# Layer-norm sources transposed in halves beside the projection lanes, and score maxima turned by products with the identity

## The chip, the cores and the metric

The kernel runs on one core of a Trainium2 chip. The metric is the time of one execution on the device in microseconds. The engines are called by their names in the profile: PE (TensorE), PEld (its weight loads), DVE (VectorE), ACT (ScalarE), POOL (GpSimd), SP (SyncE, which here only issues DMAs). All times are in microseconds where nothing else is said.

## The reference

One transformer block (PixArt) over a batch of 16, with 256 tokens and 256 features, 16 heads of 16 features:

```python
c_proj = silu(c) @ W_mod + b_mod
shift_a, scale_a, gate_a, shift_m, scale_m, gate_m = split(c_proj, 6)
q, k, v = heads(modulate(ln(x), shift_a, scale_a) @ W_qkv + b_qkv)
a = softmax(q @ k.T * hd ** -0.5) @ v
x = x + gate_a * (a @ W_proj + b_proj)
q_c = heads(ln(x) @ W_qc + b_qc)
k_c, v_c = heads(ln(context) @ W_kvc + b_kvc)
x = x + (softmax(q_c @ k_c.T * hd ** -0.5) @ v_c) @ W_cproj + b_cproj
h = gelu(modulate(ln(x), shift_m, scale_m) @ W_mlp1 + b_mlp1)
x = x + gate_m * (h @ W_mlp2 + b_mlp2)
```

Everything is float32. Most products split an operand into a rounded high part and a low remainder (both fp32r) and add three products.

## The kernel before, in words

The work after a set-up is 32 attention **units** (lines 790 to 805), 16 of self attention (kind "s") and 16 of cross attention (kind "c"). The first five and every second one up to number 25 are self attention, the others, and the last five, are cross attention. After them comes the MLP, which the change doesn't touch.

Each unit is done in eight **beats**; `beat(n, k)` (line 1103) writes out, engine by engine, what beat k of unit n issues. The order on every engine is the order of the program. PE's work in a beat:

- `visit` (line 1079): first the scores of the *next* unit (tile `s`, two pairs of matmuls of 63 rows, which sit in the two row halves of the array and run side by side). DVE takes their row maxima with one reduction (`s_tile`, line 697). There are two banks for the scores, and both are filled in each beat. Then the scores of this unit, turned (tile `st`, two pairs with 64 rows, `t_part`), which ACT exponentiates into `pt` (`exp`, line 752). Row 63 of `q` holds the negated maxima, so that `st` is already reduced by them.
- In beats 0, 2, 4 and 6 the values: `av_part` (line 771), eight products with 32 columns each, float32, that go to four column groups of the array.
- In beats 1, 3, 5 and 7 twelve pairs of projection steps, `lanes` (line 471): two matmuls side by side, one in each row half, for two projections (of Q, K, V of later units and the output projection of an earlier one). Each projection needs two lanes, one of each half, in two different beats.
- In between the transposes. `transposed` (line 377) turns a normalized source of 256 tokens by four whole-array transposes of 128 by 128, two for each half of the features. `m_turn` (line 728) turns 16 columns of maxima by one transpose, ACT negates and copies them (`m_row`, line 735), and one DMA on SP writes them into row 63 of `q`.

So a unit's maxima are turned in two halves, in beat 4 of the unit before it and in its own beat 0. The source of unit n + 3 is turned in beat 0 (two transposes, in one bank with the maxima) and beat 2 (two). Where unit n + 3 is a cross unit, its second source (`psT_q`) has all four in beat 4, and the maxima use bank `st`.

Three PSUM banks of tag "tr" go round (line 67): in a unit they serve in turn the source, a projection, the values, the second source or the maxima, a projection, the values. A fourth ("gen") holds projections by tokens, and two pairs hold `s` and `st`.

DVE's order in a beat is the maximum, then the remainders: l_k or l_kc in beat 0, l_q or l_qc in beat 4 (`low`, line 507), `xTl_s` in beat 3, `xTl_q` in beat 7, and the statistics of the layer norms. On SP in beat 0 stand the high parts of K, then the pull of the sums `S`, then the maxima, then the low part of K; in beat 4 the high parts of Q, the maxima, the low part of Q.

All instructions are recorded under line 51 of the profile, since a helper issues them. They are told apart by their tiles.

Of the kernel before, what the change touches and what calls it, by code (L numbers as in the profile page):

```python
# [10 lines left out]
F32 = mybir.dt.float32  # L11
F32R = mybir.dt.float32r
AF = mybir.ActivationFunctionType
ALU = mybir.AluOpType
# [7 lines left out]
def pixart_block(  # L22
# [53 lines left out]
    DVE.memset(wz, 0.0)  # L76
    ident = const.tile([P, P], F32, name="ident")
    make_identity(nc, ident)
    mhalf = const.tile([P, 2], F32, name="mhalf")
    POOL.memset(mhalf, -0.5)  # L80

    def gap(pool, n, name):

        pool.tile([P, n // 4], F32, tag=name, name=name, bufs=1)
# [292 lines left out]
    def transposed(src, name, scale=None, pool=False):  # L377

        o = Box()

        def place():
            o.ps = ps_gen(f"psT_{name}", SHORT)

        def turn(fs=range(KC)):
            if len(fs) == KC:
                place()
            for f in fs:
                for t in range(NT):
                    PE.transpose(o.ps[:, f * N + t * P:f * N + (t + 1) * P],
                                 src()[:, t, f * P:(f + 1) * P], ident)  # L390

        def high():
            hi = work.tile([P, KC, N], F32R, tag="xTh", name=f"xTh_{name}", bufs=4)
            lo = work.tile([P, KC, N], F32R, tag="xTl", name=f"xTl_{name}", bufs=4)
            o.xT = (hi, lo)
            if scale is None:
                ACT.copy(hi.rearrange("p k n -> p (k n)"), o.ps)
            else:
                for f in range(KC):
                    ACT.activation(hi[:, f], o.ps[:, f * N:(f + 1) * N], AF.Identity, scale=scale[f])  # L400

        def low():
            hi, lo = o.xT
            if scale is None:
                DVE.tensor_tensor(lo.rearrange("p k n -> p (k n)"), o.ps,
                                  hi.rearrange("p k n -> p (k n)"), ALU.subtract)
            else:
                for f in range(KC):
                    DVE.scalar_tensor_tensor(lo[:, f], o.ps[:, f * N:(f + 1) * N], scale[f],
                                             hi[:, f], ALU.mult, ALU.subtract)  # L410

        def full():
            o.y = work.tile([P, KC, N], F32, tag="y", name=f"y_{name}", bufs=1)
            if scale is None:
                ACT.copy(o.y.rearrange("p k n -> p (k n)"), o.ps)
            else:
# [54 lines left out]
    def lanes(x, y):  # L471


        if x:
            x.ps, x.fresh = ps_gen(f"ps_{x.name}", LONG if x.tok else SHORT), True
        return zip_longest(*(lane(o, half) for half, o in enumerate((x, y)) if o))

    def run(steps, n=12):
        for _ in islice(steps, n):
# [2 lines left out]
    def to_stack(W, src, bias, dst, which, name):  # L482
# [24 lines left out]
        def low():  # L507
            if name == "k0":
                gap(work, 64, "gap_l")
            o.lo = work.tile([P, KC, N], F32R, tag="qkl", name=f"l_{name}", bufs=3)  # L510
            if name == "k0":
                gap(work, 192, "gap_mx")
            for f in range(KC):
                DVE.scalar_tensor_tensor(o.lo[:, f], o.ps[:, f * N:(f + 1) * N], bias[f], o.hi[:, f],
                                         ALU.add, ALU.subtract)
# [181 lines left out]
    def s_tile(u, g, par, t, bank=None, home=sp):  # L697
# [12 lines left out]
            if j == 0:  # L710
                yield
        if u.mx is None:
            u.mx = work.tile([P, 2, 2, 4, NT], F32, tag="mx", name=f"mx_{u.n}", bufs=3)
# [14 lines left out]
    def m_turn(u, hf, pst=None):  # L728

        if pst is None:  # L730
            pst = ps_gen(f"psm_{u.n}_{hf}", SHORT)
        PE.transpose(pst[:16, :P], u.mx[:, hf].rearrange("p r a t -> p (r a t)"), ident)
        return pst

    def m_row(u, hf, pst):

# [31 lines left out]
            for f in pieces:  # L768
                next(f)

    def av_part(u, g):
# [8 lines left out]
        if g == 3:  # L780
            o_out(u, 1)

    def o_out(u, half):
# [295 lines left out]
    def visit(n, k, home=sp, between=None):  # L1079
# [13 lines left out]
        in_turn(*t)  # L1093
        later.append(lambda: exp(units[n], k))

    def spare(n, gate=True):
        p1, _, p3 = (v and v.post for v in map(unit, (n - 1, n - 2, n - 3)))
        if p3 and not p3.added:
            p3.add()
        if p1 and gate:  # L1100
            p1.gate()

    def beat(n, k):
# [20 lines left out]
        if k == 6:  # L1124
            if q2 and not n:
                q2.V.keep()
            if p2 and not alone:
                p2.end()
        kp = None
        if k == 5 and lx and n:  # L1130
            kp = lanes(q3.K, None if alone else p2)
        visit(n, k, between=kp and (lambda: run(kp, 2)))
        if k == 0:
            exps()
            if prev:
                av_part(prev, 3)
            if q3 and q3.ready:
                q3.T[0].place()
                pst = m_turn(cur, 1, q3.T[0].ps[:, N:])
                q3.T[0].turn((0,))  # L1140
            else:
                pst = m_turn(cur, 1)
            if prev:
                p1.pull_sums(1)
            m_row(cur, 1, pst)
            if q2:
                q2.K.low()
                q2.K.send_low()
# [3 lines left out]
                p2.low()  # L1152
        elif k == 1:
            exps()
            run(lanes(q2 and q2.Q, q2 and n and q2.V))
            if prev:
                p1.pull_values(1)
            if lc:
# [6 lines left out]
        elif k == 2:  # L1165
            exps()
            if cur:
                av_part(cur, 0)
            if q3:
                q3.T[0].turn((1,) if q3.ready else (0, 1))  # L1170
            if ls:
                ls.ln[0].steps[0]()
            elif prev:
# [24 lines left out]
        elif k == 4:  # L1198
            exps()
            if alone:  # L1200
                p2.end()
            if cur:
                av_part(cur, 1)
            if lx:
                lx.T[1].turn()
            if nxt:
                m_part(nxt, 0, st[:, 0] if lx else None)
            if q2:
                q2.Q.low()
                q2.Q.send_low()  # L1210
# [7 lines left out]
                ls.ready = True  # L1218
        elif k == 5:
            exps()  # L1220
            run(kp or lanes(q3 and q3.K, (None if alone else p2) if n else q2.V))
            if cur:
                o_out(cur, 0)
            if lc:
# [8 lines left out]
        elif k == 6:  # L1233
# [6 lines left out]
                cur.post.pull(0)  # L1240
            if q3 and p2:
                q3.vk = lanes(q3.V, q3.K)
                run(q3.vk, 1)
            if p3:
                p3.store()
            if lx:
# [126 lines left out]
```

## Time and profile before

| | us |
|---|---|
| median of 3 runs | 719.43 |
| lowest and highest run | 718.43, 721.32 |
| span of the profiled execution | 719.7 |
| PE busy | 710.4 |
| DVE busy | 567.8 |
| ACT busy | 551.7 |
| POOL busy | 520.6 |

The span is the time from the first to the last instruction of the execution that was profiled; it is the only time that this execution has, and it lies within the three runs. PE's ends are modelled, so its 99% does not say that it is at its peak. A row of the timeline is: start, time, engine, line, operation, out<-in, shapes, count, and in brackets the idle time before it. A form such as 64*128 is the part of the array that a matmul uses, rows by columns: 63*128 and 64*128 are half the rows, 128*32 a quarter of the columns, 128*128 the whole. The matmuls of a row that stands for several have started one after another; a pair in two row halves starts nearly together.

### The profile page before, as it was taken

The numbers are of one execution on the slowest core, as the hardware profiler recorded it, in microseconds if no ns is written. First come the engines' busy times: TensorE is split into PE (matmuls) and PEld (weight loads), VectorE is DVE, ScalarE is ACT, GpSimd is POOL, SyncE is SP. The second block draws the span as 40 slices with busy tenths as digits, with TensorE's granted clock in tenths as the row PEclk, the third lists the DMA queues.
The fourth block names the chain that finished last, engine by engine and source line by source line (L and its number), as shares of the span: only waits on it lengthen the run. The fifth ranks groups of instructions, "written<-read, shape, count | busy, mean of one in ns | idle before, by whom it ended". The sixth has DMA issues, their size and how long they took to land.

```text
span 719.7 us, 22488 instructions
## 1 busy us (share of the span) xinstructions
PE 710.4 (99%) x8993; PEld 592.3 (82%) x8993; DVE 567.8 (79%) x895; ACT 551.7 (77%) x955; POOL 520.6 (72%) x518
## 2 busy tenths in 40 slices
PE   9999999999999999999999999999999999999997
PEld 8777777777877778777787777777779999999997
DVE  5878888888888798888888888888675777777653
ACT  5677888888888788887888888887867677666661
POOL 7655778787776867776686798977857988656651
PEclk9999999999999999999999999999999999999999
DMA  7574455554545456454655656456323132313212
GB/s 236 183 233 157 160 170 178 175 179 160 167 151 196 162 176 191 163 166 153 195 167 176 210 174 195 156 192 196 95 78 103 59 87 61 88 46 88 66 39 74
DMA packets 81548, 106.15 MB, mean 147 GB/s; under 512 B 16610, under 2 KB 44548, under 8 KB 81444
## 3 DMA queue, kind: packets, MB, share of 16 engines
q1 hardware_dynamic: 80548, 104.37, 45.5%
q8 instruction: 71, 1.16, 0.7%
q10 hardware_dynamic: 896, 0.35, 0.2%
q14 instruction: 33, 0.27, 0.1%
HBM read 35.89 MB, written 8.98 MB: 62 GB/s over the span
## 4 chain that ended last, share of the span: by engine, by line
PE 94%; DVE 3%; POOL 2%; issue 0%; ACT 0%; POOLq 0%; ACTq 0%
PE s L51 18%; PE o L51 16%; PE st L51 16%; PE ph L51 12%; PE ps_qc L51 4%; PE ps_kc L51 4%; PE ps_k L51 4%; PE ps_q L51 3%; PE ps_v_c L51 3%; PE ps_v_s L51 3%; PE ps_P_s L51 2%; DVE mx L51 2%; PE ps_P_c L51 2%; PE psT_c L51 2%; PE psT_s L51 2%; PE psT_q L51 1%
## 5 line engine op out<-in xcount | busy, mean ns | idle before, releaser
L51 DVE TENSOR_REDUCE mx<-s 128x4 f32<-128x1024 f32 x252 | 307.9, 1222 | 73.5 <-PE s L51 70.1
L51 ACT ACTIVATE pt<-st 128x1024 f32<-128x1024 f32 x256 | 263.4, 1029 | 51.8 <-PE st L51 51.0
L51 PE MATMUL o<-pt,v 128*32 128x256 f32 x2048 | 137.1, 385 | 0.0
L51 PE MATMUL s<-big 63*128 63x256 f32 x1008 | 116.8, 305 | 1.7 <-DVE st_q L51 0.8
L51 PE MATMUL st<-big 64*128 64x256 f32 (+1 forms) x1040 | 107.7, 282 | 0.8 <-issue 0.4
L51 PE MATMUL ph<-xTh_m,wself 128*128 128x256 f32 x512 | 100.2, 281 | 0.0
L51 POOL TENSOR_TENSOR hl<-hf,hh 128x512 fp32r<-128x512 f32 x60 | 80.1, 1350 | 20.8 <-ACT hh L51 20.8
L51 PEld LDWEIGHTS s<-big 63*128 63x128 f32 x1008 | 77.3, 185 | 21.0 <-issue 7.1
L51 PEld LDWEIGHTS o<-pt,v 128*32 128x32 f32 x2048 | 53.4, 109 | 39.5 <-ACT oT L51 1.3
L51 PEld LDWEIGHTS st<-big 64*128 64x128 f32 (+1 forms) x1040 | 81.2, 186 | 3.6 <-ACT pt L51 1.5
L51 PEld LDWEIGHTS ph<-xTh_m,wself 128*128 128x128 f32 x512 | 82.3, 188 | 1.2 <-issue 0.4
L51 PE MATMUL ph<-xTl_m,wself 128*128 128x256 f32 x256 | 71.1, 278 | 0.0
L51 ACT ACTIVATE hf<-ph,bT 128x256 f32<-128x256 f32 x112 | 47.0, 473 | 22.1 <-PE ph L51 21.9
L51 ACT ACTIVATE hh<-ph,bT 128x256 fp32r<-128x256 f32 x112 | 47.0, 472 | 19.8 <-PE st L51 8.4
L51 PEld LDWEIGHTS ph<-xTl_m,wself 128*128 128x128 f32 x256 | 48.2, 188 | 0.0
L51 PE MATMUL s<-big,hh 128*128 128x256 f32 x256 | 45.6, 278 | 0.0
L51 DVE TENSOR_SCALAR xn_m<-x,mv_m,rs_m 128x256 f32<-128x256 f32 x28 | 33.5, 1237 | 14.8 <-POOL rs_m L51 14.8
L51 POOL TENSOR_SCALAR xn_q<-x,mv_q,rs_q 128x256 f32<-128x256 f32 x32 | 38.9, 1225 | 1.7
L51 POOL TENSOR_SCALAR xn_c<-c,mv_c,rs_c 128x256 f32<-128x256 f32 x32 | 38.9, 1226 | 1.7
L51 PE MATMUL st<-big,hh 128*128 128x256 f32 x224 | 40.0, 278 | 0.0
L51 PEld LDWEIGHTS s<-big,hh 128*128 128x128 f32 x256 | 38.8, 188 | 0.0
L51 POOL TENSOR_SCALAR rs_c<-mv_c 128x2 f32<-128x2 f32 x16 | 3.6, 228 | 48.3 <-DVE mv_c L51 48.2
(230 smaller groups left out, 2133.1 us busy)
## 6 DMA issues: line engine op xcount, KB each, us to landing
big<-h_k SPq DMA_DIRECT2D x32, 256.0 KB
big<-h_kc SPq DMA_DIRECT2D x32, 256.0 KB
big<-h_qc SPq DMA_DIRECT2D x32, 256.0 KB
big<-h_q SPq DMA_DIRECT2D x30, 256.0 KB
big<-l_k SPq DMA_DIRECT2D x16, 256.0 KB
g<-gd SPq DMA_DIRECT2D x16, 256.0 KB
U_s<-oT SPq DMA_DIRECT2D x32, 128.0 KB
R_s<-rd_s SPq DMA_DIRECT2D x16, 256.0 KB
```

Of the source, the lines that this page charges most:

```text
L51: i = f(*a, **k)
```

## The change

It does five things.

1. `half(h)` of a source: four transposes of 64 tokens by 128 features, in one row half of the array, instead of whole ones. `turning` issues four of them with two steps of the lane that uses the other row half: transpose, lane, transpose, transpose, lane, transpose.
2. The first half of a source stands at the head of beat 1 (second source: beat 5), ahead of the scores; the second half between `s` and `st` of the next beat. The lanes of beat 1 and 5 then run ten pairs. In beat 5 of such units no pairs stand between `s` and `st` any more.
3. The maxima are turned by `m_cols`: two products with the identity, with 32 columns (16 of them zero), ahead of the values in beats 0 and 4. They go into the bank of the source that is turned next, where there is one.
4. `m_send`: DVE negates and copies 64 by 64 of them, and two DMAs of 64 queries each write them, ahead of the copy of the values and the pull of the sums.
5. Where the second source is turned, beat 6 issues no pair of the next lanes after the values (before: one), and beat 7 all twelve.

The tile of maxima becomes a fixed one of 32 columns, cleared once, and a gap in memory is widened so that what follows stays in place. Unit 0's source stays as it was.

```diff
+    mxs = const.tile([P, 3, 2, 32], F32, name="mxs")
+    POOL.memset(mxs, 0.0)
+    mxs = [mxs[:, i] for i in range(3)]
...
+        def half(h):
+            rows = slice(64 * h, 64 * h + 64)
+            for f in range(KC):
+                for t in range(NT):
+                    c = f * N + t * P + 64 * h
+                    PE.transpose(o.ps[:, c:c + 64], src()[rows, t, f * P:(f + 1) * P], ident[rows, rows])
+                    yield
...
+    def pair_of(x, y):
+        return [lane(o, half) if o else iter(()) for half, o in enumerate((x, y))]
+    def turning(T, h, beside):
+        t = T.half(h)
+        for f in (t, beside, t, t, beside, t):
+            next(f)
...
-                gap(work, 192, "gap_mx")
+                gap(work, 576, "gap_mx")
...
+    def m_cols(u, hf, pst=None):
+        if pst is None:
+            pst = ps_gen(f"psm_{u.n}_{hf}", SHORT)
+        w = mxs[u.n % 3][:, hf]
+        for j in range(2):
+            PE.matmul(pst[32 * j:32 * j + 32, :64], w, ident[:, 64 * j:64 * j + 64], start=True, stop=True,
+                      tile_position=(0, 32 * j))
+        return pst
+    def m_send(u, hf, pst):
+        m = work.tile([64, 64], F32R, tag="m2", name=f"m2_{u.n}_{hf}", bufs=1)
+        DVE.tensor_scalar(m, pst[:64, :64], -1.0, None, ALU.mult)
+        for j in range(2):
+            SP.dma_start(u.q[63:P:64, 4 * hf:4 * hf + 4].rearrange("r a (t q) -> r a t q", t=NT)[..., 64 * j:64 * j + 64].bitcast(F32),
+                         m[32 * j:32 * j + 16].bitcast(F32))
...
-        kp = None
-        if k == 5 and lx and n:
-            kp = lanes(q3.K, None if alone else p2)
-        visit(n, k, between=kp and (lambda: run(kp, 2)))
+        between = None
+        if k in (1, 5):
+            x, y, T = ((q2 and q2.Q, q2 and n and q2.V, q3 and q3.ready and q3.T[0]) if k == 1 else
+                       (q3 and q3.K, (None if alone else p2) if n else q2.V, lx and lx.T[1]))
+            if x:
+                x.ps, x.fresh = ps_gen(f"ps_{x.name}", LONG if x.tok else SHORT), True
+            a, b = pair_of(x, y)
+            steps = weave(a, b)
+            if T:
+                held.append((T, a))
+                turning(T, 0, b)
+        elif held:
+            between = lambda: turning(held[0][0], 1, held.pop()[1])
+        visit(n, k, between=between)
+        def rest_of():
+            run(steps, 10 if held else 12)
         if k == 0:
             exps()
+            T = q3 and q3.ready and q3.T[0]
+            if T:
+                T.place()
+            pst = m_cols(cur, 1, T.ps if T else None)
             if prev:
-                av_part(prev, 3)
-            if q3 and q3.ready:
-                q3.T[0].place()
-                pst = m_turn(cur, 1, q3.T[0].ps[:, N:])
-                q3.T[0].turn((0,))
-            else:
-                pst = m_turn(cur, 1)
+                av_part(prev, 3, False)
+            m_send(cur, 1, pst)
             if prev:
+                o_out(prev, 1)
                 p1.pull_sums(1)
-            m_row(cur, 1, pst)
...
-            if q3:
-                q3.T[0].turn((1,) if q3.ready else (0, 1))
+            if q3 and not q3.ready:
+                q3.T[0].turn()
...
+            if lx:
+                lx.T[1].place()
+            if nxt:
+                pst = m_cols(nxt, 0, lx.T[1].ps if lx else None)
             if cur:
                 av_part(cur, 1)
-            if lx:
-                lx.T[1].turn()
             if nxt:
-                m_part(nxt, 0, st[:, 0] if lx else None)
+                m_send(nxt, 0, pst)
...
-                run(q3.vk, 1)
+                run(q3.vk, 0 if lx else 1)
```

More of the change, by code (lines that the diff above doesn't have):

```diff
@@ L390, in turn @@
                                  src()[:, t, f * P:(f + 1) * P], ident)
+        def half(h):
[5 more added lines that the diff above has]
+                    yield
+        o.half = half
         def high():
@@ L475, in lanes, with weave @@
             x.ps, x.fresh = ps_gen(f"ps_{x.name}", LONG if x.tok else SHORT), True
-        return zip_longest(*(lane(o, half) for half, o in enumerate((x, y)) if o))
+        return weave(*pair_of(x, y))
+    def pair_of(x, y):
+        return [lane(o, half) if o else iter(()) for half, o in enumerate((x, y))]
+    def weave(*gens):
+        return zip_longest(*gens)
+    def turning(T, h, beside):
+        t = T.half(h)
+        for f in (t, beside, t, t, beside, t):
+            next(f)
     def run(steps, n=12):
@@ L712, in s_tile @@
         if u.mx is None:
-            u.mx = work.tile([P, 2, 2, 4, NT], F32, tag="mx", name=f"mx_{u.n}", bufs=3)
+            u.mx = mxs[u.n % 3][:, :, :16].rearrange("p f (r a t) -> p f r a t", r=2, t=NT)
         mx = u.mx.rearrange("p f r a t -> p r f a t")
@@ L769, in in_turn, with av_part @@
                 next(f)
-    def av_part(u, g):
+    def av_part(u, g, out=True):
         if g % 2 == 0:
@@ L779, in av_part @@
                           start=(c == 0), stop=(c == NT - 1), tile_position=(0, h * 32))
-        if g == 3:
+        if g == 3 and out:
             o_out(u, 1)
@@ L1094, in visit @@
         later.append(lambda: exp(units[n], k))
+    held = []
     def spare(n, gate=True):
@@ L1154, in beat @@
             exps()
-            run(lanes(q2 and q2.Q, q2 and n and q2.V))
+            rest_of()
             if prev:
@@ L1220, in beat @@
             exps()
-            run(kp or lanes(q3 and q3.K, (None if alone else p2) if n else q2.V))
+            rest_of()
             if cur:
```

## The prediction

> **What bounds the kernel now.** I read the page first, then the timeline of TensorE through two units in the steady part, then the timelines of VectorE and of the weight loads beside it.
>
> ```profile
> span 719.7 us, 22488 instructions
> ...
> PE 710.4 (99%) x8993; PEld 592.3 (82%) x8993; DVE 567.8 (79%) x895; ACT 551.7 (77%) x955; POOL 520.6 (72%) x518
> ...
> PE 94%; DVE 3%; POOL 2%; issue 0%; ACT 0%; POOLq 0%; ACTq 0%
> ```
>
> TensorE is busy 99% of the span, and the chain is 94% TensorE. But ends of matmuls are modelled, so what a beat costs must be read from start to start. That is what the timeline of TensorE gives. Beats 1 to 7 of one unit whose look-ahead unit is a cross one (a "c unit" below, 16 of them), then beat 0 of the next unit, then beats 4 and 5 of that next one (an "s unit", 12 of them with the early transposes):
>
> ```profile
> 300.93 0.51 PE L51 MATMUL s<-big 63*128 63x256 f32 x4
> ...
> 302.93 0.43 PE L51 MATMUL s<-big 63*128 63x256 f32 x4
> 303.17 0.42 PE L51 MATMUL st<-big 64*128 64x256 f32 x4
> 303.52 1.07 PE L51 MATMUL o<-pt,v 128*32 128x256 f32 x16
> 304.53 0.44 PE L51 MATMUL psT_c<-ident,xn_c 128*128 128x128 f32 x2
> 304.90 0.50 PE L51 MATMUL s<-big 63*128 63x256 f32 x4
> 305.24 0.41 PE L51 MATMUL st<-big 64*128 64x256 f32 x4
> 306.85 0.42 PE L51 MATMUL s<-big 63*128 63x256 f32 x4
> 307.43 1.07 PE L51 MATMUL o<-pt,v 128*32 128x256 f32 x16
> ...
> 309.16 0.51 PE L51 MATMUL s<-big 63*128 63x256 f32 x4
> ...
> 311.11 0.42 PE L51 MATMUL s<-big 63*128 63x256 f32 x4
> 311.73 1.07 PE L51 MATMUL o<-pt,v 128*32 128x256 f32 x16
> 312.96 0.40 PE L51 MATMUL s<-big 63*128 63x256 f32 x4
> ...
> 314.74 0.45 PE L51 MATMUL s<-big 63*128 63x256 f32 x4
> 315.35 1.07 PE L51 MATMUL o<-pt,v 128*32 128x256 f32 x16
> ...
> 316.78 0.50 PE L51 MATMUL s<-big 63*128 63x256 f32 x4
> ...
> 322.72 0.41 PE L51 MATMUL s<-big 63*128 63x256 f32 x4
> 323.30 1.07 PE L51 MATMUL o<-pt,v 128*32 128x256 f32 x16
> 324.51 0.51 PE L51 MATMUL s<-big 63*128 63x256 f32 x4
> ...
> 326.47 0.44 PE L51 MATMUL s<-big 63*128 63x256 f32 x4
> ```
>
> A beat runs from one group of scores (s) to the next. So now: beat 0 is 314.74 to 316.78, 2.04; beat 1 2.00; beat 2 1.97; beat 3 1.95; beat 4 2.31 in a c unit and 1.79 in an s unit; beat 5 1.95; beat 6 1.85; beat 7 1.78. Beats with a whole-array transpose are long because the array changes its form twice. The last four value products of beat 2, and the same place in beat 6 where no transpose follows:
>
> ```profile
> 304.20 0.40 PE L51 MATMUL o<-pt,v 128*32 128x256 f32 x4
> ```
> ```profile
> 312.73 0.38 PE L51 MATMUL ps_v_c<-wvch,xTh_c 64*128 64x256 f32 x1
> ```
>
> From 304.20 to the transpose are 0.33, to the scores another 0.37. In beat 6 the values start at 311.73 and the next half-array product comes 1.00 later, as the transpose does from 303.52 to 304.53 (1.01): leaving the values costs 0.33 whatever follows. A transpose between them is therefore paid in full, with its second change of form.
>
> The second bound is behind it:
>
> ```profile
> 314.68 0.30 PEld L51 LDWEIGHTS s<-big 63*128 63x128 f32 x4
> ```
> ```profile
> 313.40 1.23 DVE L51 TENSOR_REDUCE mx<-s 128x4 f32<-128x1024 f32 x1 [0.61 <-PE s L51]
> ...
> 315.23 1.22 DVE L51 TENSOR_REDUCE mx<-s 128x4 f32<-128x1024 f32 x1
> 316.37 0.87 DVE L51 SCALAR_TENSOR_TENSOR l_kc<-ps_kc,bP,h_kc 128x256 fp32r<-128x256 f32 x2
> ```
>
> The maximum ends at 313.40 + 1.23 = 314.63 and the next scores' weights load 0.05 later, the matmul at 314.74. The two score banks are free only then. So no beat can be shorter than scores to maximum 0.44, the maximum 1.23, load and start 0.11: 1.78, and 1.85 in beat 6; I take 1.81 as the **floor**. Beats 6 and 7 stand on it now.
>
> **The change part by part.** Only starts count. One settled pair of half-array products takes 0.115: from 305.24 to 306.85 are fourteen.
>
> *Removed.* The two half-transposes at beats 0 and 2, the four of beat 4 in c units, the maxima's transpose at beats 0 and 4: with them the second change of form.
>
> *Moved in, the turnings* (line 389's transposes in halves): each is four transposes of 64 columns with two products of the other lane, once at the head of beats 1 (and 5 in c units), once between scores and second scores of beats 2 (and 6). The trace shows no such form. Nearest are whole transposes among products of the late part, where no form changes:
>
> ```profile
> 548.60 0.28 PE L51 MATMUL s<-big,hl 128*128 128x256 f32 x1
> 548.72 0.60 PE L51 MATMUL psT_m<-ident,xn_m 128*128 128x128 f32 x4
> 549.08 0.36 PE L51 MATMUL ph<-xTh_m,wself 128*128 128x256 f32 x1
> 549.28 0.28 PE L51 MATMUL ph<-xTl_m,wself 128*128 128x256 f32 x1
> ```
>
> Six starts from 548.60 to 549.28: 0.11 each, so a transpose of 128 columns costs 0.11 and mixing costs nothing; half the columns 0.055, four 0.22. Two products take 0.23 on the other half. Lower end: 0.23, the transposes all beside the products. At the head the first weight load is bare, as after every change of form (304.90 to 305.24 is 0.34, settled 302.93 to 303.17 is 0.24): 0.10 + 0.23 = **0.34** in place of that bare load at the scores; between the scores **0.26**, since one transpose trails. Upper end: each transpose with its own load, 0.45. The two products taken from beats 1 and 5 shorten those by 0.23.
>
> *Added, maxima as products*: two products with 32 columns, in the form of the values, ahead of them. The change into that form (0.35 after the second scores' start) is paid already. The price is unseen. The values' load is the row for it:
>
> ```profile
> L51 PEld LDWEIGHTS o<-pt,v 128*32 128x32 f32 x2048 | 53.4, 109 | 39.5 <-ACT oT L51 1.3
> L51 DVE SCALAR_TENSOR_TENSOR l_k<-ps_k,bqkv,h_k 128x256 fp32r<-128x256 f32 x32 | 13.9, 475 | 0.0
> L51 DVE SCALAR_TENSOR_TENSOR bqkv<-st,bP 128x32 f32<-128x32 f32 x2 | 0.4, 191 | 0.7 <-PE st L51 0.7
> ```
>
> Sixteen matmuls stand for eight products, so each runs in two passes: two loads of 0.11, **0.23**; ends 0.11 (a quarter of the values' columns) and 0.44 (four bare loads).
>
> *Moved, the copy* of the maxima from ScalarE to VectorE, between the maximum and l_k or l_q. 32 columns take 0.19, 256 take 0.475; 64 by a line between them: **0.23**, ends 0.19 and 0.475. Successive VectorE work overlaps by 0.08 (316.37 against 315.23 + 1.22), so its occupancy is 0.15. It adds a wait: the maxima now lie in the bank the turning writes, so the turning at the head of beat 1 or 5 waits for the copy, and every score behind it in TensorE's order.
>
> *Queues.* Each half's row goes out in two DMAs instead of one on SP; they now stand ahead of the sums' pull, and l_k and l_q leave later by one more issue, about 0.55 by this row:
>
> ```profile
> 310.86 0.54 SPq L51 DMA_DIRECT2D big<-l_q  x1
> ```
>
> l_q is needed by the scores at 314.74, 3.3 after its issue ended; 2.8 are left, and no TensorE row here waits for a DMA. The maxima are needed four beats later. I cost both at nothing; without that slack it would be 0.55 a unit. ScalarE gives up 0.27 twice a unit, off the path; POOL gets one early memset.
>
> *Sum by beat, c unit.* Beat 0: scores to values 0.61, maxima 0.23, values and change 1.01: the turning could start at 1.85. The maximum starts at 0.49, ends at 1.71, the copy at 1.71 - 0.08 + 0.23 = 1.86, seen at 1.91. Plus 0.34: 2.25, **+0.21**. Beat 1: fourteen pairs, 1.61, below the floor: 1.81, **-0.19**. Here the gain is capped: VectorE's maximum is late next. Beat 2: 0.59 + 0.26 + 1.01 = 1.86, **-0.11**. Beat 3 unchanged. Beat 4: 0.58 + 0.23 + 1.01 = 1.82; with 0.44 from scores to maximum the copy is seen at 1.86; plus 0.34: 2.20, **-0.11**. Beat 5: on the floor, **-0.14**. Beat 6: loses its pair of products, gains a turning: 0.58 + 0.26 + 1.01 = 1.85, **0**. Beat 7: twelve pairs now and a bare load, like beat 3, 1.95: **+0.17**. Together -0.17.
>
> *s unit.* Beats 0 to 2 as above, -0.09. Beats 4 and 5 hang on VectorE:
>
> ```profile
> 323.21 1.22 DVE L51 TENSOR_REDUCE mx<-s 128x4 f32<-128x1024 f32 x1
> 324.35 0.87 DVE L51 SCALAR_TENSOR_TENSOR l_qc<-ps_qc,bP,h_qc 128x256 fp32r<-128x256 f32 x2
> 325.13 1.21 DVE L51 TENSOR_REDUCE mx<-s 128x4 f32<-128x1024 f32 x1
> ```
>
> These stand end to end, and the scores at 326.47 follow 325.13 + 1.21 by 0.13: the copy pushes them by 0.15. The products at beat 4 also need the bank that VectorE reads last just ahead of 323.21 (until 323.21 + 0.08 = 323.29); they would start at 323.30, so 0.05 of waiting at most, under the same VectorE chain. Together +0.06.
>
> 16 x -0.17 + 12 x 0.06 = -2.0 us. The profiled execution's span is 719.7, which gives 717.7; the median of the runs shown is 719.43, 0.3 lower, so I forecast **717.4**.
>
> **The rivals.** *The turnings don't run beside the products* (slower). If a transpose's load can't go under a running matmul of its own half, each takes load and stream and the turning 0.45: +0.11 at beats 0 and 4, +0.19 at 2 and 6; 16 x 0.60 + 12 x 0.30 = 13.2, so **730.5**. It decides from 0.064 a turning (88 of them make the 5.6 us from forecast to slower by 0.5%). Against it: the 0.11 of whole transposes in one form, which leaves no room for a bare load. For it: no row has four loads in one half between products of the other. The Trainium skill, page TensorE: Matmul & The Clock Gate, Part 3, "What overlaps and what doesn't", says that a weight load overlaps running matmuls only where the row group differs; by that rule the time would be that 730.5. The rows at 548.72 disagree for the whole array, and no run here shows halves.
>
> *The copy is dear* (slower): at 0.475 the wait grows by 0.25 in beats 0 and 4 of c units and in beats 0 and 5 of s units, 16 x 0.50 + 12 x 0.50 = 14: **731.5**. The 32-column row speaks against it.
>
> *The transposes vanish beside the products* (faster): head 0.23, between 0.23, copy 0.19: c units gain 2 x 0.11 + 2 x 0.03 + 2 x 0.04, s units 0.11 + 0.03 + 2 x 0.04: 16 x 0.36 + 12 x 0.22 = 8.4: **709**. The bare load at 304.90 speaks against the whole of it. Below that the floor stands.
>
> **How the numbers follow.** Forecast 0.40, hidden transposes 0.34, turnings in series 0.19, dear copy 0.07. About 0.5% (3.6 us) is what a measurement can tell from no change. Faster by more: the third rival, 0.34; same: the forecast less a little spill to slower, 0.38; slower 0.28. Range for 8 in 10: 709 to 728, which takes the faster rival and turnings that are partly serial. The forecast's own range is 714.5 to 721.5.
>
> **What would show it.** Right: beat 1 at 1.81 with the scores' load 0.05 behind the maximum; beat 0 near 2.25 with the first half-transpose waiting for VectorE's copy; beat 7 of c units at 1.95; no 128*128 form left in the loop's steady part. Wrong: four half-transposes more than 0.34 from first start to the scores; the maxima's products over 0.3; a copy over 0.3; scores waiting for a DMA.

## The result, and the profile after

The changed kernel takes 722.99 us (median of 7 runs, 721.09 to 725.32), the kernel before beside it 719.43 us (7 runs). The ratio is 1.0048, with a 95% interval of 1.0031 to 1.0066: slower by a little less than 0.5%, where 717.4 us had been forecast. The time lies inside the range of 709 to 728, but on the other side of the kernel before.

The page of the changed kernel, with the lines that answer to those shown of before:

```profile
span 720.7 us, 23403 instructions
...
PE 701.6 (97%) x9358; PEld 599.6 (83%) x9358; DVE 574.8 (80%) x958; ACT 542.9 (75%) x892; POOL 520.8 (72%) x519
...
PE 73%; issue 7%; POOL 7%; DVE 7%; DMA 3%; ACT 1%; SPq 1%; DVEq 0%; ACTq 0%; POOLq 0%
```

The profiled execution took 722.46 us. TensorE's busy time went down by 8.8 us and the span did not, so time has moved from work into waits; the chain, 94% TensorE before, now leaves it for a quarter of its way. Which waits these are, the waits of the weight loads and of TensorE tell (columns: us in total, times, longest us). First the kernel before, then the changed kernel:

```profile
PEld s L51 <- DVE mx L51: 5.4, 14, 0.6
```
```profile
PEld s L51 <- DVE mxs L51: 27.1, 63, 0.6
```
```profile
PE psT_c L51 <- DVE m L51: 3.0, 15, 0.2
PE psT_q L51 <- DVE m L51: 2.8, 14, 0.2
PE psT_s L51 <- DVE m L51: 1.8, 9, 0.2
```

The scores' weights wait for the maximum 63 times instead of 14: more beats stand on the floor. And the first half-transpose waits for VectorE's copy `m`, 15 + 14 + 9 = 38 times. The timeline of TensorE through beats 0, 1 and 2 of a c unit of the changed kernel shows both places:

```profile
302.01 0.42 PE L51 MATMUL s<-big 63*128 63x256 f32 x4
302.26 0.40 PE L51 MATMUL st<-big 64*128 64x256 f32 x4
302.59 0.25 PE L51 MATMUL psT_c<-ident,mxs 128*32 128x64 f32 x2
...
302.73 1.03 PE L51 MATMUL o<-pt,v 128*32 128x256 f32 x14
303.96 0.24 PE L51 MATMUL psT_c<-ident,xn_c 64*128 64x64 f32 x1 [0.20 <-DVE m L51]
...
304.21 0.50 PE L51 MATMUL s<-big 63*128 63x256 f32 x4
304.53 0.42 PE L51 MATMUL st<-big 64*128 64x256 f32 x4
...
306.02 0.51 PE L51 MATMUL s<-big 63*128 63x256 f32 x4
306.37 0.28 PE L51 MATMUL ps_q<-xTl_s,wself 64*128 64x256 f32 x1
306.37 0.28 PE L51 MATMUL psT_c<-ident,xn_c 64*128 64x64 f32 x2
...
306.59 0.48 PE L51 MATMUL st<-big 64*128 64x256 f32 x4
307.00 1.07 PE L51 MATMUL o<-pt,v 128*32 128x256 f32 x16
308.00 0.50 PE L51 MATMUL s<-big 63*128 63x256 f32 x4
```

Beat 0 (302.01 to 304.21) is 2.20, beat 1 1.81, beat 2 1.98. Over all units, the medians of each beat from the first start of its scores to that of the next (16 c units, 12 s units; the last column belongs to an experiment below):

| beat | c before | c forecast | c after | s before | s after | c, copy on ScalarE where a turning follows |
|---|---|---|---|---|---|---|
| 0 | 2.06 | 2.25 | 2.24 | 2.04 | 2.22 | 2.02 |
| 1 | 1.99 | 1.81 | 1.82 | 2.00 | 1.82 | 1.82 |
| 2 | 1.97 | 1.86 | 1.97 | 1.95 | 1.97 | 1.97 |
| 3 | 1.95 | 1.95 | 1.97 | 1.95 | 1.96 | 1.96 |
| 4 | 2.31 | 2.20 | 2.19 | 1.79 | 1.84 | 1.97 |
| 5 | 1.97 | 1.81 | 1.82 | 1.96 | 1.98 | 1.82 |
| 6 | 1.84 | 1.85 | 1.97 | 1.84 | 1.90 | 1.97 |
| 7 | 1.79 | 1.95 | 1.97 | 1.80 | 1.80 | 1.95 |

The differences of the medians, to three places, sum to +0.064 a c unit and +0.124 a s unit: 16 x 0.064 + 12 x 0.124 = +2.5 us. All beats of the two profiled executions together, single stalls included, give +3.45 us; the medians of the runs differ by 3.56. (The two spans differ by 1.0 only, because the profiled execution of before lost some 2 us more in the part behind the beats. Every run that lists both has a span 1.7 to 1.9 us below its time, 720.7 and 722.46 here. So a span of 719.7 stands for a time of about 721.5, just above the runs shown of before and not among them.)

Beats 0, 1, 3, 4, 5 and 7 of the c units came within 0.02 of the forecast. **Beats 2 and 6 did not**: 1.97 instead of 1.86 and 1.85, in 44 places.

### The profile page after: what moved, and what is told of

Same layout as the page of the kernel before. It is cut to its first block, busy times and chain, and to the rows that moved or that the text cites. A ratio compares the mean times of both kernels' runs of the same rounds, so it can differ in the third digit from the quotient of the medians.

```text
span 720.7 us, 23403 instructions
## 1 busy us (share of the span) xinstructions
PE 701.6 (97%) x9358; PEld 599.6 (83%) x9358; DVE 574.8 (80%) x958; ACT 542.9 (75%) x892; POOL 520.8 (72%) x519
## 4 chain that ended last, share of the span: by engine, by line
PE 73%; issue 7%; POOL 7%; DVE 7%; DMA 3%; ACT 1%; SPq 1%; DVEq 0%; ACTq 0%; POOLq 0%
PE s L51 17%; PE st L51 13%; PE ph L51 12%; PE o L51 8%; DVE mxs L51 4%; PE ps_q L51 3%; PE ps_qc L51 3%; PE ps_kc L51 3%; PE ps_k L51 3%; PE ps_P_s L51 2%; PE ps_v_c L51 2%; PE ps_v_s L51 1%; PE ps_P_c L51 1%; DMA R_s<-rd_s 1%; DVE m L51 1%
## 5 line engine op out<-in xcount | busy, mean ns | idle before, releaser
L51 DVE TENSOR_REDUCE mxs<-s 128x4 f32<-128x1024 f32 x252 | 307.8, 1222 | 69.2 <-PE s L51 62.1
L51 PE MATMUL o<-pt,v 128*32 128x256 f32 x2048 | 141.4, 384 | 0.0
L51 PE MATMUL s<-big 63*128 63x256 f32 x1008 | 122.2, 313 | 2.8 <-DMA U_s<-oT 1.1
L51 PE MATMUL st<-big 64*128 64x256 f32 (+1 forms) x1040 | 111.2, 285 | 0.5 <-ACT pt L51 0.4
L51 PEld LDWEIGHTS st<-big 64*128 64x128 f32 (+1 forms) x1040 | 84.1, 186 | 3.4 <-ACT pt L51 1.3
L51 PEld LDWEIGHTS o<-pt,v 128*32 128x32 f32 x2048 | 66.7, 109 | 22.0
L51 ACT COPY oT<-o 128x512 f32<-128x512 f32 x64 | 37.5, 586 | 1.6 <-PE o L51 1.4
```

What stands on the lines that cost most here:

```text
L51: i = f(*a, **k)
```

## Experiments

Times are medians, ratios are to the kernel before on the same chip, with 95% intervals. "Lane" is one row half's series of projection steps.

### The wait for the copy: other columns

```diff
-            pst = m_cols(cur, 1, T.ps if T else None)
+            pst = m_cols(cur, 1, T.ps[:, 64:] if T else None)
-                pst = m_cols(nxt, 0, lx.T[1].ps if lx else None)
+                pst = m_cols(nxt, 0, lx.T[1].ps[:, 64:] if lx else None)
```

> Everything as in the changed kernel, but the products of the maxima go to columns 64 to 127 of the new source's bank instead of 0 to 63, so the first half-turning writes other columns than the copy reads. Theory (the first half-turning waits for the maxima's copy): the last start of the values to the first transpose falls from 0.58 to about 0.31 us, beat 0 from 2.22-2.24 to about 1.97 and beat 4 before a cross unit from 2.19 to about 1.92, 28 beats, -7.5 us: about 715.5 us; the beats behind them (1 and 5) stay at 1.82 or lose up to 0.05 each because the vector engine now has its copy in front of the low part (716.9). Rival (the copy is hidden, and what made beat 0 long is the products and the turning themselves): beats 0 and 4 stay within 0.03, about 723 us.

723.76 us, ratio 1.0062 (1.0040 to 1.0083). No beat's median moved by over 0.013. But this does not speak for the rival, since the wait was not taken away, as the waits of TensorE show:

```profile
PE psT_q L51 <- DVE m L51: 3.2, 16, 0.2
PE psT_c L51 <- DVE m L51: 3.1, 16, 0.2
PE psT_s L51 <- DVE m L51: 2.2, 11, 0.2
```

The turning writes other columns than the copy reads and waits all the same: in this program a bank is waited for as a whole. The theory had taken the columns for the unit of the wait, and was wrong in that.

### The wait for the copy: another engine

```diff
-        DVE.tensor_scalar(m, pst[:64, :64], -1.0, None, ALU.mult)
+        ACT.mul(m, pst[:64, :64], -1.0)
...
-            exps()
...
             pst = m_cols(cur, 1, T.ps if T else None)
+            m = m_send(cur, 1, pst)
+            exps()
```

(`m_send` makes the copy alone here; its DMAs stay behind the values.)

> The changed kernel with one thing undone: the maxima are copied out of the bank by the scalar engine again, but ahead of the exponential of beats 0 and 4, behind the high part of K or Q. In the changed kernel's profile the scalar engine is free for the copy some 0.6 us before the vector engine is, which must first finish the reduction of the same beat. Theory (the first half-turning waits for the copy in the whole bank): the wait goes, the last start of the values to the first transpose falls from 0.58 to about 0.31 us, beat 0 from 2.22-2.24 to about 1.97 and beat 4 before a cross unit from 2.19 to about 1.92; 28 beats, -7.5 us, 715.5 us (714 to 717); the exponential starts about 0.15 us later, which is just what the next beat leaves it. Rival (the wait isn't what makes beats 0 and 4 long; values with products and a turning are): 723 us, beats 0 and 4 within 0.03.

**714.69 us**, ratio 0.9927 (0.9907 to 0.9947): faster than the kernel before, and 8.3 us below the changed kernel (1.2% by the two ratios). Beats 0 fell by 0.24, beats 4 of c units by 0.22. These are 28 and 16 beats (the "28 beats" of the expectation is a miscount, 44 is right): -10.2 us, less what beats 5 of the s units took. Beat 4 of a c unit and the head of beat 5 on TensorE, then ScalarE in the same stretch:

```profile
305.19 0.25 PE L51 MATMUL psT_q<-ident,mxs 128*32 128x64 f32 x2
...
305.32 1.03 PE L51 MATMUL o<-pt,v 128*32 128x256 f32 x14
306.29 0.27 PE L51 MATMUL psT_q<-ident,xn_q 64*128 64x64 f32 x1
...
306.56 0.48 PE L51 MATMUL s<-big 63*128 63x256 f32 x4
```
```profile
304.85 0.85 ACT L51 ACTIVATE h_q<-ps_q,bqkv 128x256 fp32r<-128x256 f32 x2
305.59 0.22 ACT L51 ACTIVATE m<-psT_q 64x64 fp32r<-64x64 f32 x1
305.71 1.01 ACT L51 ACTIVATE pt<-st 128x1024 f32<-128x1024 f32 x1
```

From the first maxima product to the first half-transpose are 1.10 here (305.19 to 306.29) and 1.37 in the changed kernel (302.59 to 303.96). The copy is done at 305.81, half a microsecond before the turning wants the bank. In the changed kernel it could not be, because it stood behind the reduction of the same beat on VectorE:

```profile
302.47 1.23 DVE L51 TENSOR_REDUCE mxs<-s 128x4 f32<-128x1024 f32 x1
303.61 0.21 DVE L51 TENSOR_SCALAR m<-psT_c 64x64 fp32r<-64x64 f32 x1
303.74 0.86 DVE L51 SCALAR_TENSOR_TENSOR l_k<-ps_k,bqkv,h_k 128x256 fp32r<-128x256 f32 x2
304.75 1.23 DVE L51 TENSOR_REDUCE mxs<-s 128x4 f32<-128x1024 f32 x1
```

One thing was not expected: beat 5 of the s units rose by 0.21 (beat 6 gave 0.07 back). There no turning follows, and the copy ahead of the exponential only delays it. That led to the next kernel.

### The copy on ScalarE only where a turning follows

```diff
+        if act:
+            ACT.mul(m, pst[:64, :64], -1.0)
+        else:
+            DVE.tensor_scalar(m, pst[:64, :64], -1.0, None, ALU.mult)
```

> The copy of the maxima on the scalar engine ahead of the exponential, but only in the 28 beats where a half-turning follows in the same bank; in the other beats 4 (before self units, 12) the vector engine copies as in the changed kernel. Theory (the scalar copy is worth its place only where the turning waits for it; ahead of the exponential it delayed the scores of beat 5 of the self units by 0.21 each): 12 x (0.21 less 0.07 given back in beat 6) = 1.7 us less than with the scalar copy everywhere (714.7), about 713 us. Rival (beat 5 of the self units is late for another reason): 714.7 us.

714.54 us, ratio 0.9948 (0.9933 to 0.9964). Beat 5 of the s units fell by the expected 0.21, beat 6 rose by 0.07, and the medians of the beats sum to 1.4 us less than with the copy everywhere. The time of the runs did not follow to 713: the difference of the two medians, 0.15 us, is within what the runs scatter. Its profiled execution holds four stalls of 0.4 to 1.5 us at the ends of beats 7, 3.5 us in all (see the order of the transfers, below).

### The copy twice

```diff
-        DVE.tensor_scalar(m, pst[:64, :64], -1.0, None, ALU.mult)
+        for _ in range(2):
+            DVE.tensor_scalar(m, pst[:64, :64], -1.0, None, ALU.mult)
```

> The changed kernel with the copy of the maxima made twice on the vector engine (the second one writes the same numbers). Theory (the copy's end sets the start of the first half-turning): each of 28 beats 0.13 us longer (the pitch of such a copy), +3.6 us, about 726.6 us. Rival (copy hidden): 723 us.

736.6 us, ratio 1.0235 (1.0208 to 1.0262). Beats 0 (28) rose by 0.25, beats 4 of c units (16) by 0.27, beats 5 of s units (12) by 0.25: 14.3 us. TensorE's waits for the copy more than doubled:

```profile
PE psT_q L51 <- DVE m L51: 7.2, 16, 0.5
PE psT_c L51 <- DVE m L51: 6.3, 14, 0.5
PE psT_s L51 <- DVE m L51: 3.6, 8, 0.5
```

The mechanism is the theory's, the size was not: a second copy into the same tile costs 0.25 and not the pitch of 0.13, there are 44 such beats and not 28, and the 12 beats of the s units in which VectorE's work stands end to end had been left out.

### The products alone, from the kernel before

```diff
             if T:
                 T.place()
             pst = m_cols(cur, 1, T.ps[:, N:] if T else None)
             if prev:
                 av_part(prev, 3, False)
             if T:
                 T.turn((0,))
             m_send(cur, 1, pst)
```

> The kernel before with one part of the change alone: maxima by products ahead of the values and the copy on the vector engine; the sources are turned whole, where they were turned before. The products go to the second half of the source's bank. Theory (products cost about 0.10 where the whole turning of the maxima cost about as much, and no instruction of the tensor engine waits for the copy here): beats 0 and 4 within 0.05 of before, total 719 to 721 us. Rival (the copy on the vector engine is what is dear, since it stands ahead of the low parts): beats 1 and 5 longer by 0.1 or more each, 722 us or more.

749.94 us, ratio 1.0437 (1.0419 to 1.0455). The theory fell. The rival's signs came (beats 1 and 5 of c units longer, more than 722 us), but the copy is dear here for a wait, not for its length of 0.22. The bank again: the copy is issued behind the whole transposes into the same bank, so VectorE waits for TensorE, and l_k or l_q behind it. VectorE's waits, and the place in the timeline:

```profile
DVE m L51 <- PE psT_q L51: 11.1, 16, 0.7
...
DVE m L51 <- PE psT_c L51: 7.2, 15, 0.5
```
```profile
316.24 0.22 DVE L51 TENSOR_SCALAR m<-psT_c 64x64 fp32r<-64x64 f32 x1 [0.47 <-PE psT_c L51]
```

Beats 5 of c units, whose lanes between the scores wait for the bank that l_q still reads, rose by 0.92, beats 1 by 0.30. So this kernel did not measure the products. The next one, with ScalarE's early copy ahead of the transposes in the bank's order, does:

```diff
             pst = m_cols(cur, 1, T.ps[:, N:] if T else None)
+            m = m_send(cur, 1, pst, T)
+            exps()
             if prev:
                 av_part(prev, 3, False)
             if T:
                 T.turn((0,))
-            m_send(cur, 1, pst)
+            m_go(cur, 1, m)
```

(`m_send` copies, `m_go` issues the two DMAs.)

> The kernel before with the products of the maxima alone: they stand ahead of the values, sources are turned whole in their old places, and the copy is made by the scalar engine ahead of the exponential where a turning follows in the same bank. Theory (products cost as much as the whole turning of the maxima that they replace, and bring nothing by themselves; what the change brings comes from the half-turnings): beats 0 +0.04, self units' beats 4 +0.05 as in the run with the vector engine's copy, the other beats within 0.03, about +1 to +2 us on the kernel before. Rival (the products are the gain): 3 us or more below the kernel before.

723.62 us, ratio 1.0063 (1.0042 to 1.0085). The products bring nothing; they cost. The medians of the beats sum to +1.8 us (beats 0 +0.02 to +0.05, beats 4 of s units +0.06, beats 6 +0.05), as the theory had it; the rest of the 5 us is in single beats, stalls of 0.2 to 1.4 us among them, and isn't settled. This kernel and the one with ScalarE's copy where a turning follows (714.54) share the products and the copy. They differ by the half-turnings, with the pair of products moved from beat 6 to beat 7, and by the columns of the maxima. The medians of their beats sum to 9.7 us less with half-turnings. **With the copy on ScalarE the half-turnings take 9 us off; the products cost 2 to 5, and the place of the copy about 8.**

### The second half-turning: its transposes twice

```diff
-            between = lambda: turning(held[0][0], 1, held.pop()[1])
+            between = lambda: [turning(held[0][0], 1, held[0][1]), run(held.pop()[0].half(1))]
```

> The changed kernel with the transposes of the second half-turning between scores issued twice (the second time without a lane beside them, same numbers). Theory (a half transpose takes its pitch of 0.06 us, as in the trace, and the rest of what beat 2 and 6 gained is the form in which the scores stand): each of 44 beats about 0.24 us longer, +10.5 us, about 733.5 us. Rival (the rows of one half in series, 0.11 us for each transpose that has no partner): 0.44 us a beat, 742 us. If they cost nothing where they are: 723 us.

736.48 us, ratio 1.0231 (1.0205 to 1.0256). Beats 2 and 6 rose by 0.248, 44 times: 10.9 us of the 13.5. Stalls at the ends of beats 7 are 4.7 us in its profiled execution, 2.5 in that of the changed kernel. Eight half-transposes of beat 2:

```profile
314.51 0.50 PE L51 MATMUL s<-big 63*128 63x256 f32 x4
...
314.85 0.28 PE L51 MATMUL psT_c<-ident,xn_c 64*128 64x64 f32 x2
...
314.97 0.35 PE L51 MATMUL psT_c<-ident,xn_c 64*128 64x64 f32 x3
315.10 0.38 PE L51 MATMUL st<-big 64*128 64x256 f32 x1
315.16 0.35 PE L51 MATMUL psT_c<-ident,xn_c 64*128 64x64 f32 x3
315.32 0.48 PE L51 MATMUL st<-big 64*128 64x256 f32 x3
```

0.062 for a half-transpose with four of them in one row half and no partner beside: they are not in series with their loads. So the turnings in series of the prediction are ruled out, and what beats 2 and 6 have too long is not there.

### The second half-turning later

```diff
-        elif held:
-            between = lambda: turning(held[0][0], 1, held.pop()[1])
+        elif held and k in (3, 7):
+            x, y = (p2 if n else q2.V, q2.Q) if k == 3 else (q3.V, q3.K)
...
+            turning(held.pop(), 1, a)
...
-            run(steps, 10 if held else 12)
+            run(steps)
```

(The new place is ahead of that beat's scores.)

> The changed kernel with the second half-turnings moved from between the scores of beats 2 and 6 to the head of beats 3 and 7, beside two steps of that beat's own lane; beats 1 and 5 run their lanes to the end, so two steps of a lane stand alone there, and two in beats 3 and 7. Theory (what beats 2 and 6 got too long is in part the bare load of their scores, 0.07 to 0.09, which follows from beats 1 and 5 standing on their floor, and not the place of the turning): beat 1 rises from 1.82 to about 1.97, beat 2 falls from 1.97 to about 1.85 with its scores' first-to-last start at about 0.15 in place of 0.23, beat 3 stays or rises by up to 0.1: 724 to 727 us. Rival (the place between scores is dear: 0.38 where a head takes 0.26): beats 2 and 6 fall with nothing given back, about 717 us.

722.93 us, ratio 1.0036 (1.0014 to 1.0057): no different from the changed kernel. Point by point both missed. Beat 1 stayed at 1.82 instead of rising to 1.97; beat 2 fell to 1.95 only; beats 3 and 7 fell to 1.80, on the floor; beats 4 rose by 0.11 to 0.13 and beats 0 by 0.04 to 0.08. The timeline tells why beats 1 and 3 are so short:

```profile
308.39 0.39 PE L51 MATMUL s<-big 63*128 63x256 f32 x1
308.41 0.27 PE L51 MATMUL ps_q<-xTl_s,wself 64*128 64x256 f32 x1
308.52 0.40 PE L51 MATMUL s<-big 63*128 63x256 f32 x3
```

A lane step without a partner runs beside the first scores, which use the other row half. It isn't free, it is paid in the next beat: from 308.39 the scores take 0.25 to their last start (0.14 in beat 4 of the changed kernel's c units).

The same move on top of ScalarE's copy:

> As with the scalar copy in 28 beats, and with the second half-turnings at the head of beats 3 and 7 beside two steps of that beat's own lane. In the changed kernel that move took 0.16 from beats 3 and 7 and gave 0.11 to 0.13 back in beats 4 and 0.04 to 0.08 in beats 0. Theory (steps of a lane without a partner run beside the scores and cost little, so the move saves about 0.05 for each of 44 turnings): 710 to 712 us. Rival (all of it is given back in the beats behind): 713 us.

718.25 us, ratio 0.9987 (0.9969 to 1.0004), some 4 us worse than without the move, though its runs scatter from 714.1 to 720.5 and the medians of its beats sum to 2.1 us more. Theory and rival both fell: beats 3 and 7 gave 0.16, beats 2 and 6 took 0.09 to 0.11, beats 4 and 0 up to 0.12. With the copy on ScalarE the place between the scores is the better one.

### One more pair, three more pairs

Zero weights, so that the added products add nothing (the second kernel runs over three such pairs):

```diff
             run(steps, 10 if held else 12)
+            if held:
+                for o, rows in ((x, slice(0, 64)), (y, slice(64, P))):
+                    PE.matmul(o.ps[:, :N], wz[rows].bitcast(F32R), o.src.xT[0][rows, 0], start=False, stop=False,
+                              skip_group_check=True)
```

> The changed kernel with one more pair of lane matmuls (with zero weights, adding nothing) at the end of beats 1 and 5 where a half-turning was made. Theory (those beats stand on their floor of 1.82, with some 0.08 of the tensor engine idle ahead of the next scores, whose weights then load bare, 0.229 from first to last start in place of 0.15): beats 1 and 5 rise by 0.03 or less, beats 2 and 6 fall by 0.05 to 0.08 to about 1.90, in all -1 to -2 us, 721 to 722 us. Rival (beats 1 and 5 aren't on a floor, and a bare load isn't what made beat 2 long): a pair costs its pitch of 0.11, 44 times, +4.8 us, about 728 us, beats 2 and 6 unchanged.

721.14 us, ratio 1.0040 (1.0024 to 1.0056). Adding 44 pairs of 0.11 cost nothing that can be measured: beats 1 and 5 rose by 0.01 to 0.02. They stand on the floor. But beats 2 and 6 fell by 0.02 only, since the scores still waited for the maximum. So this run showed the floor and left the second half of the theory open; hence the other one:

> The changed kernel with three more pairs of lane matmuls (zero weights) at the end of beats 1 and 5 where a half-turning was made, so that these beats surely stand above their floor. One such pair cost 0.01 to 0.02 a beat and left the next scores' load waiting. Theory (a beat that follows a floored beat pays 0.07 for the bare load of its scores): beats 1 and 5 rise by 0.24 (two pairs at 0.113 behind the free one), beats 2 and 6 fall by 0.07 to about 1.90; in all +7.5 us, about 730.5 us. Rival (beats 2 and 6 are long for the turning alone): they stay at 1.97, +10.7 us, about 733.5 us.

728.37 us, ratio 1.0125 (1.0100 to 1.0150). Beats 1 and 5 rose by 0.25, and beats 2 and 6 **fell by 0.07 to 0.08**, to 1.89 and 1.90: the theory's numbers. Beat 2 of this kernel, then the weight loads of its scores here and in the changed kernel:

```profile
310.31 0.45 PE L51 MATMUL s<-big 63*128 63x256 f32 x4
310.55 0.28 PE L51 MATMUL ps_q<-xTl_s,wself 64*128 64x256 f32 x1
310.60 0.28 PE L51 MATMUL psT_c<-ident,xn_c 64*128 64x64 f32 x2
...
310.79 0.50 PE L51 MATMUL st<-big 64*128 64x256 f32 x4
```

```profile
310.19 0.35 PEld L51 LDWEIGHTS s<-big 63*128 63x128 f32 x4
```
```profile
306.02 0.30 PEld L51 LDWEIGHTS s<-big 63*128 63x128 f32 x4
```

Here the loads begin 0.12 ahead of the first score, while the lanes still run; in the changed kernel they begin with it, at 306.02, and the maximum that they waited for ended at 304.75 + 1.23 = 305.98. From the first to the last start of the four scores of beat 2 it is 0.14 here and 0.23 in the changed kernel (medians). The lane step follows the scores' start by 0.24 here, by 0.35 in the changed kernel (306.02 to 306.37), with the same turning behind it. Where the beat ahead has work for TensorE to its end, the scores' weights are loaded under it; where it ends in a wait for the maximum, both pairs of loads stand bare.

### The order of the transfers

The profiled execution of the changed kernel has three stalls at the end of beats 7, of 0.37, 1.26 and 0.90 us. At 80.99 the scores of unit 3's first beat are late:

```profile
80.99 0.50 PE L51 MATMUL s<-big 63*128 63x256 f32 x4 [1.13 <-DMA U_s<-oT]
```
```profile
74.61 1.17 SPq L51 DMA_DIRECT2D big<-m  x2
75.83 0.57 SPq L51 DMA_DIRECT2D big<-l_q  x1
```

They need l_q, which SP issues behind the two transfers of the maxima. Fifteen of its sixteen parts landed by 78.21, the last at 80.79. (The row names another transfer that ended close by; the weights' loads go on 0.1 after the last part of l_q. In the other two stalls the last part of the low part of Q was late as well: 64.11 with fifteen parts there at 62.26, and 113.24 with fifteen at 111.17, each 0.1 ahead of the scores.)

```diff
-                m_send(nxt, 0, pst)
+                m = m_send(nxt, 0, pst)
             if q2:
                 q2.Q.low()
                 q2.Q.send_low()
+            if nxt:
+                m_go(nxt, 0, m)
```

(`m_send` copies, `m_go` issues the two DMAs; the same in beat 0 with K.)

> The changed kernel with the low part of K and of Q computed and sent ahead of the two small transfers of the maxima (the copy on the vector engine stays first). Theory (the low part of Q leaves some 0.55 us later in the changed kernel, so that it is late for the scores in a few units: stalls of 0.37, 1.26 and 0.90 us in the profile): the stalls at the end of beat 7 are fewer and smaller, the median is 1 to 2 us below the changed kernel, 721 to 722, with the beats' medians unchanged. Rival (these stalls come from transfers that are late whatever the order): 723 us, stalls as before.

722.97 us, ratio 1.0062 (1.0044 to 1.0080). The stalls at beat 7 all but went (one of 0.17 is left), others of 0.2 to 0.7 us came in beats 3, and the sum of all beats is the same to 0.1 us. So the theory that the order costs the changed kernel 1 to 2 us falls. Together with the other columns:

> Both edits: maxima at columns 64 to 127, and the low parts sent ahead of the maxima. Theory: the two gains add up, about 714.5 us (713 to 716), faster than both kernels by 0.5 to 0.9%. Rival (the time taken from beats 0 and 4 comes back as waits for the low parts or for the reductions of the next beat): above 717 us.

723.94 us, ratio 1.0074 (1.0060 to 1.0088), like the changed kernel, which fits two edits neither of which changes the time. Why one part in sixteen of a transfer sometimes lands 2.6 us late stays open.

## Why the prediction was wrong

**The floor** was right. Beats 1 and 5 came at 1.82 against 1.81, the scores' loads wait for the maximum (306.02 behind 305.98, above), and another pair of products in them costs 0.01 to 0.02.

**The head** (the maxima's products, the wait for their copy and the half-turning ahead of the scores), right in its sum, which was luck, and not in its parts. Beat 0 was put at 2.25 and came at 2.24, beat 4 of c units at 2.20 and 2.19. But the maxima's products were put at 0.23 and cost 0.09 to 0.10: with the wait taken away, 1.10 from the first of them to the half-transpose against 1.01 for values alone. The copy was expected to be seen 0.06 after the turning could start, and was seen 0.27 after (1.37 against 1.10). From the first half-transpose to the scores are 0.25 (303.96 to 304.21), not 0.34; the bare load that the 0.34 held shows behind the scores' start, in beat 1. So 0.10 + 0.27 + 0.25 = 0.62 stands for 0.23 + 0.06 + 0.34 = 0.63. The copy's own length was well put, 0.21 against 0.23, and so was its end, 1.80 to 1.85 after the scores' start against 1.86; its wait was not, since the turning could start 0.12 earlier than forecast and saw the copy 0.15 after its end instead of 0.05. Hidden in a right sum, the wait was worth 0.22 to 0.24 in 44 beats, and it was the one term that could be had back by a better place.

**The step that failed**: "Beat 2: 0.59 + 0.26 + 1.01 = 1.86", and likewise beat 6. Both came at 1.97. From the first score to the first value 0.59 + 0.26 = 0.85 was forecast and 0.97 measured. The 0.59 was taken from beats before which TensorE had work to the end. By the prediction's own account beats 1 and 5 stand on the floor, so the scores after them start on a wait, with bare loads: 0.07 to 0.08, shown by the three pairs. The remaining 0.03 to 0.05 lie on the turning (from the scores' first start to the values 0.89 to 0.90 in that run, against 0.85 forecast). The step mis-sized one beat, by not asking what the beat before had become. (For beat 6 the prediction used 0.58, which is its reading of beat 4; the rows that it shows for beat 6, 311.11 and 311.73, give 0.62. In the changed kernel beats 2 and 6 are alike, 0.97.) In numbers: 16 x (0.114 + 0.139) + 12 x 0.129 = 5.6 us.

**The rest** nearly cancels: beats 0 0.03 to 0.04 shorter than forecast (-1.0), beats 4 and 5 of s units 0.07 instead of 0.15 (-1.0), beats 6 of s units +0.05 (+0.6), the others +0.3. So -2.0 + 5.6 - 1.1 is +2.5, the sum of the medians. The last microsecond is in stalls (2.5 us in the profile after, 1.7 in the one before), which vary from run to run. Scores that wait for a DMA, one of the prediction's signs of being wrong, are in the three stalls at the ends of beats 7; the term put at nothing, transfers of l_q that leave later, was not shown to cost anything, since the time stayed at 722.97 with l_q sent first.

**The rivals.** Turnings in series (0.45 each): ruled out, by the 0.062 of a half-transpose without a partner. The rule that the prediction weighed, of the Trainium skill, page TensorE: Matmul & The Clock Gate, Part 3, "What overlaps and what doesn't", by which a load overlaps only matmuls of other row groups, doesn't hold here: eight half-transposes of one row half start within 0.43 us in the run with the doubled turning, though each of their loads is shown with 0.14, over two starts long. Hidden transposes: not so either, as the head takes 0.25 from the half-transpose to the scores and leaves their loads bare. A dear copy: its length was not 0.475. But the kernel did come out slower, and the copy's place is a large part of why: with the copy taken to ScalarE the same turnings and products give 714.7 us.

## What to carry to other kernels

When a beat is put on a floor, price the next beat anew: what used to load under its predecessor's tail now loads after the wait. Before giving a copy to an engine, ask not how long the copy is but what that engine must finish first; here the engine with the same 0.2 us copy and a free slot half a microsecond earlier turned a loss of 0.5% into a gain of 0.5 to 0.7%. And a sum that comes out right beat by beat can still hide two wrong terms, which only an experiment on one of them shows.

## What was not expected of the hardware

- Half-transposes in one row half start 0.06 apart, beside a lane step of the other half or without one, and mixing them with half-array products adds no change of form: four of them with two lane steps take 0.25 to the scores (303.96 to 304.21), where going from the values to two whole transposes and on to the scores took 0.33 + 0.37.
- A lane step that has no partner runs beside the scores of the other row half: 308.39 and 308.41 in the run with the later turning.
- A second copy of 64 by 64 into the same tile on VectorE adds 0.25 us, where two different instructions in a row overlap to a pitch of 0.13 (303.61 to 303.74).
